# A four-layer graph network on one core: projections of layer 0's second step taken before its weighted sums, another split of the first group, and later projections in layers 1 and 2

## The chip, the core and the metric

The kernel runs on one core of a Trainium2 chip. The core has five engines that work side by side, each through its own instructions in order: TensorE (PE, matrix products and transposes), VectorE (DVE), ScalarE (ACT), GpSimd (POOL), and SyncE (SP), which here issues every transfer between the chip's memory and the core. An instruction that waits holds up all that stands behind it on its engine, and the same is true of SP's queue of transfers.

The metric is the time of one execution on the device in microseconds. The kernel before took 3104.74 us, the median of three runs (3103.69, 3104.74 and 3111.75).

## The reference

A graph of 3327 nodes with 256 features and a weighted adjacency matrix goes through four layers, each `x = x + layer(relu(layernorm(x)), adj)`. The change is mainly in layer 0:

```python
R = S + eye; R = R / R.sum(-1, keepdims=True)
Z = 0; Xf = X; Xa = X
for n in range(2):
    A = top_p_attention(Xa, W1, W2, W3)   # row softmax, the largest entries up to mass 0.9, renormalised
    Xf = R @ Xf
    Xa = A @ Xa
    Z = Z + Xf @ U1[n].T + Xa @ U2[n].T
h = X + Z
return layernorm(h) * ln_g + ln_b
```

Layer 1 is `relu(tanh(adj * adj) @ (tanh(h @ W_proj + b) @ W_gcn) + b_gcn)`, the mask and the limit of 700 entries a row changing nothing for such data. Layers 2 and 3 are graph attention: `Wh = h @ W`, scores from two columns of `Wh @ a`, a softmax over the neighbours, and a product with `Wh`. Everything is float32.

## The kernel before

The nodes are padded to 26 tiles of 128 rows. The matrix `adj` is at hand as it is and as transposed blocks `adj_t`.

**Layer 0** (function `layer0`) runs its two steps one after the other, and in each step the 26 tiles in nine groups of up to three (`FG`). For a group (function `group`):

- *Scores*: eight matrix products a tile (L1042) with the keys `kt` and a query that SP loads from `q_d`; DVE copies them from PSUM with a running maximum (L1016), ACT takes the exponential (L1025).
- *Threshold search*: a first guess (L1085 on DVE), then four rounds. In a round the mass above a candidate threshold is summed over a whole row of 3328: on DVE in one pass (L1131), or on ACT in two (L1126, Relu and Sign, with sums). `ON_ACT = [2, 2, 1, 2]` says how many of the three tiles ACT takes in each round. Some ten small DVE operations (L1137 to L1158) then give the next threshold.
- *Final*: two more DVE passes and a maximum of eight a tile (L1173, L1176, L1187).
- `weighted` for each tile: transposes of the probabilities (L951), copies by ACT (L953), 26 products with the rows `xa` (L941) into `ps_out`; ACT multiplies by the norm (L963). The result and the row of `R @ Xf`, loaded from `xf_d` as `xf_in`, are transposed (`turned`, L785, L786) and multiplied with `u1s` and `u2s` (L971) into `ps_row`; DVE adds what the row has so far (`h` in step 1, `base_row` loaded from `zz_d` in step 2, L979) and the sum is stored to `zz_d`. In step 1 the transposed result also gives the keys and query of step 2 (`keys_of`, L858). Also in step 1, a triple that depends on nothing of it: a tile of `x` is loaded, the bias `ln_b` is added on POOL, and the sum is stored to `xb_d` for layer 1 (L989 to L991, one buffer).

Beside the groups run the *neighbour tiles* (`neighbours`): four block loads of `adj_t` a tile (L906), 26 products (L915) into the single `ps_acc`, a scaling on ACT (L923), a store to `xf_d` or `xf2_d`. In step 1 ACT also takes the sign of each block (L909, one buffer `sg`) and SP stores it to `sign_d` for the later layers. Step 2 takes its `xf` from `xf_d` by two large loads (L1230).

All of this is written as Python generators. `overlapped` starts a new group every 20 ticks and advances every running generator by one `yield` a tick; a scheduler then places the instructions engine by engine by its own model of their times, so that program order and engine order differ. In the first group of a step no other group is at hand to fill in.

**Layer 1** goes over the 26 tiles: two block loads, a DVE and an ACT pass, 26 products (L1482), then `summed` for the tile before and `entered2` for the one before that, which is `Entry.tile_in`: normalise on ACT (L1400), transpose on PE (L785), copy by ACT (L786), product with `w2l` (L1405), two copies (L1409, L1410). `Entry.__init__` computes a bound of the scores (`shift`) on PE, DVE and POOL (L1376 to L1385). Layers 2 and 3 are two calls of `attention`; while layer 2 runs, works in `todo` do the same `tile_in` for layer 3.

Of the kernel before, what the change touches and what calls it, by code (L numbers as in the profile page):

```python
# [20 lines left out]
P = 128  # L21
# [45 lines left out]
def kernel(  # L67
# [107 lines left out]
    xf2_d = dram.tile([NP, D], F32, name="xf2_d")  # L175
    xb_d = dram.tile([NP, D], F32, name="xb_d")
# [569 lines left out]
    def layers(fast):  # L746
# [54 lines left out]
        def layer0(wp, mp, ap_, tp, sp):  # L801
# [43 lines left out]
            def u_tiles(s):  # L845
                pair = []
                for u, name in ((u1t, "u1s"), (u2t, "u2s")):
                    t = wp.tile([P, 2, D], F32, tag=name, name=name)
                    nc.sync.dma_start(t, u[s].rearrange("(c p) n -> p c n", p=P))
                    pair.append(t)  # L850
# [31 lines left out]
            for span in spans:  # L882
# [7 lines left out]
                for k, it in enumerate(span):  # L890
# [3 lines left out]
                    keys_of(turned(row, "xt", 2), 0, it)  # L894
# [4 lines left out]
            def neighbours(s, it, xf):  # L899

                acc = ps_acc()
                w = XW if s == 0 else D
                for chunks in QB:
# [3 lines left out]
                    if s == 0:  # L907
                        sg = tp.tile([P, 7, P], I8, tag="sg", bufs=1, name="sg")
# [14 lines left out]
                nc.scalar.mul(row, acc[:, :D], rr[:, it : it + 1])  # L923
                nc.sync.dma_start((xf_d, xf2_d)[s][it * P : (it + 1) * P, :], row)
                yield

            def weighted(s, it, e, norm, xa, xa_next, us):

                if s == 0:
                    base = h(it)[:, :D]  # L930
                else:
                    base = tp.tile([P, D], F32, tag="base", bufs=1, name="base_row")
                    nc.sync.dma_start(base, zz_d[it * P : (it + 1) * P, :])
                xf_in = tp.tile([P, D], F32, tag="xf_in", name="xf_in")
# [24 lines left out]
                if s == 0:  # L959
                    row = xa_next(it)[:, :D]  # L960
                else:
                    row = tp.tile([P, D], F32, tag="xa_row", bufs=1, name="xa_row")
                nc.scalar.mul(row, po, norm)  # L963
                yield
                xt = turned(row, "xt", 2)
                xft = turned(xf_in, "xft", 2)
                yield
                pz = ps_row()
                for n, (lhs, u) in enumerate(((xft, us[0]), (xt, us[1]))):
# [5 lines left out]
                if s == 0:  # L975
                    keys_of(xt, 1, it)
                yield
                zrow = tp.tile([P, D], F32, tag="zrow", bufs=1, name="zrow")
                nc.vector.tensor_tensor(zrow, pz[:, :D], base, ALU.add)  # L979
                nc.sync.dma_start(zz_d[it * P : (it + 1) * P, :], zrow)  # L980
                if s == 1:
                    norm_of(zrow, sp, "mv_z", mv_z[:, it, :])
                yield
                if s == 0:

# [467 lines left out]
        with tc.tile_pool(name="l1", bufs=2, reuse_waits="tile") as l1:  # L1453
# [15 lines left out]
            for it in range(NT):  # L1469
# [17 lines left out]
                if it >= 2:  # L1487
                    entered2(it - 2)
# [246 lines left out]
```

## Time and profile before

| | |
|---|---|
| median of three runs | 3104.74 us |
| the profiled execution, its own time | 3100.91 us |
| its span, first to last instruction | 3099.1 us |
| layer 0, step 1: last product with `h` ends | about 1017 us |
| layer 0, step 2: last product with `xa` ends | about 1999 us |
| layer 1: products with `gw` | about 1999 to 2343 us |
| layers 2 and 3 | about 2343 to 3099 us |
| mean granted clock of TensorE | 0.973 |

The profile is one execution on the chip. It has the busy time of each engine; the span in 40 slices, each digit the busy tenths of one slice; the chain of work that ended last, followed back from the end; groups of instructions by source line; and waits by who released them. The times of the trace are microseconds from the start of the span. In lines of instructions the first number is the start, the second the length, then engine, line, operation, output and inputs; what stands in brackets is the idle time before, and what ended it. Each matrix product in float32 shows as two records, so that 26 products count as 52.

### The profile page before, as it was taken

To read this page: it belongs to the slowest core of one execution; us is meant where nothing else is said; L and a number is where in the kernel's file an instruction comes from. 1 tells how busy PE (TensorE), PEld (TensorE's weight loads), DVE (VectorE), ACT (ScalarE), POOL (GpSimd) and SP (SyncE) were. 2 spreads that over 40 slices of the span, in tenths; PEclk is the share of its full clock that TensorE was granted. 3 is DMA by queue.
4 is the path that set the end of the run, shared out by engine and by line. 5 is a ranking of instruction groups with operands and counts; after the bars stand their busy time and mean duration, and the time that the engine had idled before them with its cause. 6 is when DMAs were issued, how large, how long until landed. Compare 5 with 4: busy or idle time off the path is not lost.

```text
span 3099.1 us, 37681 instructions
## 1 busy us (share of the span) xinstructions
PE 2823.0 (91%) x13454; PEld 2277.8 (73%) x13454; DVE 2370.4 (76%) x4133; ACT 1979.7 (64%) x2633; POOL 417.8 (13%) x742
## 2 busy tenths in 40 slices
PE   7788899999999899999999988999997999979998
PEld 5466677777778576667777767888886887758887
DVE  3678889778874588889876858377765999769996
ACT  6767787768773566687666555433334777657776
POOL 0120010000001001111110024211110333210000
PEclk9889999999999999999999989999998999989999
DMA  4431112321242231211232231388871211112221
GB/s 138 131 102 45 55 45 76 95 78 57 75 121 87 73 103 53 64 35 54 74 90 72 83 114 60 105 321 318 324 243 32 71 59 59 30 48 78 75 74 37
DMA packets 183035, 298.83 MB, mean 96 GB/s; under 512 B 24701, under 2 KB 137016, under 8 KB 179512
## 3 DMA queue, kind: packets, MB, share of 16 engines
q1 hardware_dynamic: 182838, 296.34, 30.3%
q8 instruction: 108, 1.77, 0.3%
q14 instruction: 89, 0.72, 0.1%
HBM read 251.97 MB, written 44.30 MB: 96 GB/s over the span
## 4 chain that ended last, share of the span: by engine, by line
DVE 38%; PE 27%; ACT 16%; issue 8%; DMA 7%; POOL 3%; SPq 0%; ACTq 0%; POOLq 0%; DVEq 0%
ACT junk_a L1126 9%; PE ps_wide L1594 5%; DVE below L1173 4%; PE ps_out L941 4%; PE ps_acc L915 4%; DVE w L1176 4%; PE ps_wide L1482 4%; DVE below L1131 3%; DVE e L1187 3%; DVE places L1601 3%; DVE places L1587 2%; DVE below L1085 2%; DVE places L1588 2%; DMA blk<-in_adj_t 2%; DMA adj_rows<-in_adj 2%
## 5 line engine op out<-in xcount | busy, mean ns | idle before, releaser
L1126 ACT ACTIVATE junk_a<-e,minus 128x3328 int8<-128x3328 f32 x208 | 638.8, 3071 | 3.7
L1594 PE MATMUL ps_wide<-wh,places 128*128 128x257 f32 x1872 | 451.2, 383 | 35.6 <-DVE places L1588 32.7
L1594 PEld LDWEIGHTS ps_wide<-wh,places 128*128 128x128 f32 x1872 | 353.3, 191 | 93.6 <-ACT places L1586 16.5
L915 PE MATMUL ps_acc<-h,blk 128*128 128x258 f32 x1352 | 333.3, 399 | 46.8 <-ACT xf_row L923 37.1
L915 PEld LDWEIGHTS ps_acc<-h,blk 128*128 128x128 f32 x1352 | 261.8, 198 | 102.3 <-ACT xf_row L923 42.7
L1016 DVE TENSOR_SCALAR_CACHE_REDUCE e<-ps_wide 128x1024 f32<-128x1024 f32 (+1 forms) x176 | 178.6, 1019 | 206.9 <-PE ps_wide L1042 206.4
L915 PE MATMUL ps_acc<-xf,blk 128*128 128x256 f32 x1352 | 312.9, 384 | 14.3 <-ACT xf_row L923 14.2
L941 PE MATMUL ps_out<-h,wt 128*128 128x256 f32 x1352 | 311.2, 381 | 4.7 <-ACT wt L953 4.7
L941 PE MATMUL ps_out<-xa,wt 128*128 128x256 f32 x1352 | 311.9, 381 | 0.9 <-ACT wt L953 0.7
L1585 ACT ACTIVATE places<-places,sd 128x512 f32<-128x512 f32 (+1 forms) x364 | 246.3, 684 | 100.5 <-PE ps_wide L1594 67.6
L1482 PE MATMUL ps_wide<-gw,blk 128*128 128x256 f32 x1352 | 300.9, 379 | 1.3 <-ACT blk L1479 1.3
L915 PEld LDWEIGHTS ps_acc<-xf,blk 128*128 128x128 f32 x1352 | 253.9, 191 | 61.8 <-ACT xf_row L923 19.3
L1482 PEld LDWEIGHTS ps_wide<-gw,blk 128*128 128x128 f32 x1352 | 254.5, 190 | 35.0 <-ACT blk L1479 1.7
L941 PEld LDWEIGHTS ps_out<-h,wt 128*128 128x128 f32 x1352 | 249.8, 190 | 40.1 <-ACT wt L953 6.3
L941 PEld LDWEIGHTS ps_out<-xa,wt 128*128 128x128 f32 x1352 | 249.4, 190 | 34.8 <-ACT wt L953 3.0
L1586 ACT ACTIVATE places<-places,d 128x512 f32<-128x512 f32 (+1 forms) x364 | 235.8, 682 | 48.7 <-DVE places L1587 48.2
L1131 DVE SCALAR_TENSOR_TENSOR below<-e,v 128x3328 f32<-128x3328 f32 x72 | 265.3, 3684 | 1.8
L1587 DVE TENSOR_TENSOR places<-places,places 128x1024 f32<-128x1024 f32 (+1 forms) x182 | 210.2, 1163 | 65.8 <-ACT places L1585 63.7
L1042 PE MATMUL ps_wide<-keys,q 64*128 64x512 f32 (+1 forms) x832 | 215.9, 570 | 17.8 <-DVE e L1016 14.8
L953 ACT COPY wt<-ps_wide 128x1024 f32<-128x1024 f32 x208 | 175.2, 846 | 86.2 <-PE ps_wide L951 85.6
L1588 DVE SCALAR_TENSOR_TENSOR places<-blk_s,places 128x1024 f32<-128x1024 int8 (+1 forms) x182 | 206.3, 1142 | 2.0
L1176 DVE MAX8 w<-below 128x8 f32<-128x3328 f32 x52 | 188.3, 3621 | 0.3
(275 smaller groups left out, 4312.6 us busy)
## 6 DMA issues: line engine op xcount, KB each, us to landing
blk<-in_adj_t SPq DMA_DIRECT2D x104, 448.0 KB, 3.5
blk<-in_adj_t SPq DMA_DIRECT2D x52, 832.0 KB, 7.1
adj_rows<-in_adj SPq DMA_DIRECT2D x25, 1663.5 KB, 8.4
blk<-in_adj_t SPq DMA_DIRECT2D x104, 384.0 KB, 3.3
blk_s<-sign_d SPq DMA_DIRECT2D x72, 256.0 KB, 2.9
blk_s<-pos_d SPq DMA_DIRECT2D x44, 416.0 KB, 3.6
pos_d<-pos SPq DMA_DIRECT2D x22, 416.0 KB, 2.9
xf_d<-xf_row SPq DMA_DIRECT2D x52, 128.0 KB, 2.4
```

The source lines that it names most:

```text
L915: nc.tensor.matmul(acc[:, :w], blk[:, j, :], xf(jc)[:, :w], start=(jc == 0), stop=(jc == NT - 1))
L941: nc.tensor.matmul(po, wt[:, k * P : (k + 1) * P], xa(jc)[:, :D], start=(jc == 0), stop=(jc == NT - 1))
L1042: nc.tensor.matmul(pl[:, f * 512 : f * 512 + cw], q[f * DA : (f + 1) * DA, :], kt[f * DA : (f + 1) * DA, s, c0 : c0 + cw], start=True, sto ...
L1126: nc.scalar.activation(junk, es[i], (AF.Relu, AF.Sign)[n], bias=minus[:, 0, i : i + 1], accum_out=(ga, sa)[n][:, 0, i : i + 1],)
L1131: nc.vector.scalar_tensor_tensor(below, es[i], v[:, 3, i : i + 1], es[i], ALU.is_ge, ALU.mult, accum_out=v[:, 1, i : i + 1],)
L1176: nc.vector.max(w9[:, i, 1:9], below)
L1482: nc.tensor.matmul(po, filt[:, j * P : (j + 1) * P], gw(jc), start=(jc == 0), stop=(jc == NT - 1))
L1585: nc.scalar.activation(e1[:, :, q, :], s0, AF.Exp, bias=sd[:, jc + q, 1:2])
L1586: nc.scalar.activation(e2[:, :, q, :], s1, AF.Exp, bias=d2[:, jc + q : jc + q + 1])
L1587: nc.vector.tensor_tensor(e1, e1, e2, ALU.max)
L1588: nc.vector.scalar_tensor_tensor(e1, signs[:, :n, j : j + 2, :], 0.0, e1, ALU.is_gt, ALU.min)
L1594: nc.tensor.matmul(pos_[k], e1[:, k, q, :], wh(jc + q)[:, : D + 1], start=(jc + q == 0), stop=(eye and jc + q == NT - 1),)
```

## The change

In step 1, `weighted` now multiplies the transposed rows also with the U1 and U2 of step 2 (a second product `py`), stores the one result to `xfu_d` and keeps the other as the rows `xa` of step 2; both pairs of U stay in memory. Step 2 then needs no transposes and no projection: `neighbours` adds the row of `zz_d` to its scaled row on POOL, and `weighted` ends with one DVE operation, `po * norm + xf_in`. The xb triple moves to the end of `neighbours` in step 2. The signs have two buffers, `xt`, `xft` and `xf_in` one each. In a step's first group ACT takes at most one tile a round. `Entry.tile_in` is split into `turned` and `projected`, with a tile between them; the score bound becomes a method, `shifted`, called later.

```diff
             def neighbours(s, it, xf):
...
+                if s == 1:
+                    base = tp.tile([P, D], F32, tag="xf_in", bufs=1, name="base_row")
+                    nc.sync.dma_start(base, zz_d[it * P : (it + 1) * P, :])
...
-                        sg = tp.tile([P, 7, P], I8, tag="sg", bufs=1, name="sg")
+                        sg = tp.tile([P, 7, P], I8, tag="sg", name="sg")
...
                 nc.scalar.mul(row, acc[:, :D], rr[:, it : it + 1])
+                if s == 1:
+                    nc.gpsimd.tensor_tensor(row, row, base, ALU.add)
                 nc.sync.dma_start((xf_d, xf2_d)[s][it * P : (it + 1) * P, :], row)
                 yield
+                if s == 1:
+                    xb = tp.tile([P, D], F32, tag="xt", bufs=1, name="xb")
+                    r = rows_of(it)
+                    for a, b in rows_to_load(it):
+                        nc.sync.dma_start(xb[a:b], x[it * P + a : it * P + b])
+                    nc.gpsimd.tensor_tensor(xb[:r], xb[:r], b_b[0][:r], ALU.add)
+                    nc.sync.dma_start(xb_d[it * P : it * P + r, :], xb[:r])

             def weighted(s, it, e, norm, xa, xa_next, us):
...
+                zrow = tp.tile([P, D], F32, tag="zrow", bufs=1, name="zrow")
+                if s == 1:
+                    yield
+                    nc.vector.scalar_tensor_tensor(zrow, po, norm, xf_in, ALU.mult, ALU.add)
+                    nc.sync.dma_start(zz_d[it * P : (it + 1) * P, :], zrow)
+                    norm_of(zrow, sp, "mv_z", mv_z[:, it, :])
+                    yield
+                    return
...
-                for n, (lhs, u) in enumerate(((xft, us[0]), (xt, us[1]))):
+                for n, (lhs, u) in enumerate(((xft, us[0][0]), (xt, us[0][1]))):
...
+                py = ps_row()
+                for n, (lhs, u) in enumerate(((xft, us[1][0]), (xt, us[1][1]))):
+                    for cc in range(2):
+                        nc.tensor.matmul(
+                            py[:, n * D : (n + 1) * D], lhs[:, cc, :], u[:, cc, :], start=(cc == 0), stop=(cc == 1)
+                        )
                 yield
+                row = tp.tile([P, D], F32, tag="xf_row", name="xfu_row")
+                nc.scalar.copy(row, py[:, :D])
+                nc.sync.dma_start(xfu_d[it * P : (it + 1) * P, :], row)
+                nc.scalar.copy(xa_next(it), py[:, D:])
+                yield
...
-                    on_act = list(range(max(g - ON_ACT[r], g - 2 if g > 2 else 1), g)) if g > 1 else []
+                    most = 1 if tiles[0] == 0 else ON_ACT[r]
+                    on_act = list(range(max(g - most, g - 2 if g > 2 else 1), g)) if g > 1 else []
...
-                nc.sync.dma_start(t, xf_d[f * HB * P : (f + 1) * HB * P, :].rearrange("(t p) d -> p t d", p=P))
+                nc.sync.dma_start(t, xfu_d[f * HB * P : (f + 1) * HB * P, :].rearrange("(t p) d -> p t d", p=P))
...
                 if it >= 2:
-                    entered2(it - 2)
+                    entry2.turned(it - 2, xn(it - 2))
+                if it == 2:
+                    entry2.shifted()
+                if it >= 3:
+                    projected(it - 3)
...
-                    rest = [lambda it=it: following.tile_in(it, xn(it)) for it in span]
-                    todo += [stats[:2]] + [rest[k : k + 1] + stats[k + 2 : k + 3] for k in range(n)]
-                    todo.append([lambda i=i: following.spread(i)])
+                    turned = [lambda it=it: following.turned(it, xn(it)) for it in span]
+                    made = [lambda it=it: following.projected(it) for it in span]
+                    todo += [stats[:2]] + [
+                        turned[k : k + 1] + made[max(k - 1, 0) : k] + stats[k + 2 : k + 3] for k in range(n)
+                    ]
+                    todo.append(made[-1:] + [lambda i=i: following.spread(i)])
```

## The prediction

> **What bounds the kernel now.** I read the page's busy shares and slices first, then busy time in stretches of the run, then single rounds.
>
> ```profile
> PE 2823.0 (91%) x13454; PEld 2277.8 (73%) x13454; DVE 2370.4 (76%) x4133; ACT 1979.7 (64%) x2633; POOL 417.8 (13%) x742
> ...
> PE   7788899999999899999999988999997999979998
> ...
> PEclk9889999999999999999999989999998999989999
> ...
> DVE 38%; PE 27%; ACT 16%; issue 8%; DMA 7%; POOL 3%; SPq 0%; ACTq 0%; POOLq 0%; DVEq 0%
> ```
>
> TensorE is busy 2823 of 3099 us; 276 us are idle, gathered where a stage starts (the low digits, with a lower clock). The busy times between ends of groups in layer 0 (start:end, length, then PE, PEld, DVE, ACT, POOL):
>
> ```profile
> 266.00:359.00 93.00, 81.41 (x396) 61.70 (x396) 80.86 (x157) 71.88 (x77) 3.00 (x17) 0.96 0.15 43
> ...
> 560.00:665.00 105.00, 99.36 (x486) 77.42 (x485) 82.58 (x159) 78.51 (x83) 3.39 (x18) 0.98 0.26 75
> ...
> 1197.00:1290.00 93.00, 87.14 (x420) 66.51 (x420) 81.75 (x161) 66.10 (x63) 12.31 (x23) 0.98 0.19 55
> ...
> 1478.00:1579.00 101.00, 95.61 (x470) 74.57 (x469) 87.47 (x169) 67.16 (x65) 15.28 (x25) 1.00 0.23 66
> ```
>
> A group with three neighbour tiles in it is bound by PE at 95% busy; one with fewer (the first and third row) is held by DVE and PE together. So time that leaves PE counts in full only until DVE (81 to 87 us a group) is the bound. The start of step 2, one round (start, length, engine):
>
> ```profile
> 1074.80 3.69 DVE L1131 SCALAR_TENSOR_TENSOR below<-e,v 128x3328 f32<-128x3328 f32 x1
> ...
> 1088.94 0.16 DVE L1137 SCALAR_TENSOR_TENSOR sa<-sa,v 128x2 f32<-128x2 f32 x1 [8.87 <-ACT junk_a L1126]
> ```
>
> ```profile
> 1076.18 3.06 ACT L1126 ACTIVATE junk_a<-e,minus 128x3328 int8<-128x3328 f32 x1
> ...
> 1079.36 3.07 ACT L1126 ACTIVATE junk_a<-e,minus 128x3328 int8<-128x3328 f32 x1
> ...
> 1082.55 3.07 ACT L1126 ACTIVATE junk_a<-e_h,minus 128x3328 int8<-128x3328 f32 x1
> ...
> 1085.75 3.07 ACT L1126 ACTIVATE junk_a<-e_h,minus 128x3328 int8<-128x3328 f32 x1
> ```
>
> With no other group to fill in, the round is four ACT passes (13 us), while DVE does one pass and waits 8.87 us.
>
> **The first group's split (both steps).** One tile of three goes to ACT: two passes, 6.4 us, beside two DVE passes, 7.4, plus 1.9 of small operations: 9.3 us a round. In step 1 the rounds now start at 106.8, 133.0, 150.4 and 160.3 and end at 177.5. The first also holds group 1's exponentials: 26 becomes 12, the second 17.4 becomes 9.4, the third (already one) stays, the last 17 becomes 9.4. That is -30, and -2 for scores that no longer queue behind the xb transfers: the first product moves from 203.7 to about 172. In step 2 (rounds from 1056.8 to 1115.3) the gains are 4, 5, 0 and 6 us, less 3 to 5 because the second half of `xf` now waits for the last tile's projected row: -12.
>
> **What that start gives back.** In the built order of the changed kernel only 4.0 neighbour tiles stand before PE's first product in step 1; before it was 6.35, and by the ninth product the counts agree (9.8). A tile is 52 matmuls of 0.217 us, 11.3 us. So 2.35 tiles, 26.6 us of PE, move from the idle start into the PE-bound part: +28 at 95%. In step 2 it is 5.3 against 6.3, made up by the twelfth product.
>
> **Projections in step 1.** Each tile gains four matmul pairs. Their rows of step 2:
>
> ```profile
> 1152.23 0.44 PE L785 MATMUL ps_row<-ident,xa_row 128*128 128x128 f32 x2
> 1152.51 0.38 PE L785 MATMUL ps_row<-ident,xf_in 128*128 128x128 f32 x2
> ...
> 1158.21 1.13 PE L971 MATMUL ps_row<-u1s,xft 128*128 128x256 f32 x4
> 1159.18 1.03 PE L971 MATMUL ps_row<-u2s,xt 128*128 128x256 f32 x4
> ```
>
> 2.16 us x 26 = 56 us of PE, 59 at 95%. The idle left in 203 to 457 (23 us, of which 13 stay at 5%) takes up 10 to 13. The two new ACT copies a tile (0.4 us as the 128x256 copies, 22 in all) lie beside PE, ACT being at 75%; without that cover they are late releases of PSUM. The new product needs a `ps_row` bank that DVE's zrow addition frees, and that can stand behind a 3.7 us pass: 0 to +15; PE waits there are under 2 us each today, so I take +3. The extra `xfu_d` stores (2.4 us like `xf_d`) are needed only at the step's end. **Step 1: -32 +28 +59 -12 = +43.**
>
> **Step 2 without them.** Each tile loses all four rows above: 2.98 us x 26 = 77 us of PE, plus the waits for `xa_row` and `xft` (9.5 us between 1190 and 1720). DVE's work stays (one operation replaces the addition). Groups in turn, DVE taken at 94% busy, as it is between 2400 and 2600 (91.8 and 95.3) where it bounds: after the first product 62 loses 3; 93, 93 become 87 (DVE 82/0.94), -6 each; 95 gets 0.8 of a neighbour tile more, -1; 101 becomes 93 (DVE 87.5), -8; 126 and 113, PE-bound, -9 each; 121 is partly the latency of the last group and layer 1's entry, -4; the last 60, -5. With the 12: **step 2: -63.**
>
> **The xb stream.** Its 26 load-add-store triples sat in the start of step 1 on one buffer; now they stand in SP's queue at the start of step 2, about one per two block loads.
>
> ```profile
> SPq L991 <- POOL xb L990: 40.2, 14, 5.6
> ```
>
> SP waited 40 us for these additions (14 times, 5.6 at most); queued behind are block loads and thus PE. In step 1's start neighbour tiles came every 14 to 25 us, with the single-buffered signs as a second cause (now two buffers); undisturbed, every 12. In step 2 the 4.3 tiles before the first product have from about 1046 to 1121 by the old clock, room for 17 us each. Ends: 0, or 4.3 x 7 = +30. Nearer the undisturbed row, as no sign stores stand between: +4.
>
> **Additions on POOL.** 26 new row+base additions. The Trainium skill, "GPSIMD Engine Reference", sections 4.1 and 8, advises against: a two-input operation takes about twice VectorE's time and contends with VectorE instructions that have two SBUF inputs. Here the same addition takes 0.73 us (median of 26), but up to 3.04; the DVE pass at 202.03, beside one, took 4.02 against 3.69. By time on POOL, 13% busy, the sum is 0; with that 0.33 each, +9. I take +1.
>
> **The clock.** "TensorE: Matmul & The Clock Gate", Part 1, says that PE halves its clock after about 3.4 us idle and needs as much work to return: 1.7 us lost each time. It speaks against an emptier start. The row: a neighbour tile after 4.6 us idle (177.7) took 14.3 us, after 1.7 us (1103.8) 11.5. Three returns cost 8 by the trace, 5 by the rule; the four or five of today go, and the start's end is set by DVE: 0.
>
> **Later projections.**
>
> ```profile
> PE ps_row L1405 <- ACT ht L786: 10.6, 10, 2.6
> ```
>
> In layer 1 (1990 to 2330) PE, 95% busy, waits ten times for the copy of a transposed tile, 10.6 us in all. A tile's delay removes it; next to be late is the 85 to 90% busy DMA: ends 0 and -11, I take -6. In layer 2 the same wait is 8.0 us, but DVE bounds: -2 with the moved `shifted`. Both transitions (2330 to 2370, 2730 to 2765) keep their chain. Layer 3: 0. `b_b`, both u loads and the tag changes lie in idle DMA: 0.
>
> **Sum.** +43 +3 -63 +4 +1 -6 -2 = -20. The profiled execution took 3100.9 us (span 3099.1), 3.8 under the median of the runs, 3104.7. 3101 - 20 = 3081; I say 3082.
>
> **Rivals.**
> 1. *Step 1 absorbs the projections.* If the 59 us fill PE's waits (ACT is asked less in the starts, signs have two buffers, and PE idles 5% even in the full groups) half of it vanishes, -50 in all: 3050. For it: waits for `xf_row` and `xa` of 37 us in 266 to 1000. Against: these come from in-order ACT queues, which get longer.
> 2. *A wash.* Step 2 proves DVE-bound at 90 a group and the deferred tiles cost all: the -63 becomes -44, 3101.
> 3. *Slower: the xb stream stalls SP at step 2's start.* Were neighbour tiles there at 20 us or more, the first product waits for PE's queue, not for DVE: from 17 us a tile on, each microsecond costs 4.3. At 25, as the worst tile of step 1's start, (25 - 17) x 4.3 = 34 over my sum, 3115; with a bank wait of 8 in step 1, 3123.
> 4. That an edit does nothing is excluded: the built order has the 104 transposes fewer and the products moved.
>
> **Numbers.** Forecast 0.53, first rival 0.29, wash 0.09, slower 0.09. A difference under 0.3% (9 us) can't be told from none. Of the forecast 0.52 lies beyond that on the faster side and 0.01 within; of the wash 0.03 and 0.06; of the slower case 0.01 within and 0.08 beyond. Faster: 0.52 + 0.29 + 0.03 = 0.84; same 0.01 + 0.06 + 0.01 = 0.08; slower 0.08. The range reaches from the first rival, with 5 us for its bounds, 3045, to where half of the slower case begins, 3108.
>
> **What would show it.** Right: step 1's last product near 1060 (now 1016), 26 products of step 2 in about 63 us less than now; first-group rounds of 9 to 12 us; PE groups of about 110 us in step 1 and 87 to 94 in step 2; no PE wait for `ht`. Wrong: step 1 ending before 1045, SP waits for xb above 40 us together with PE waits for `blk` in step 2, or step 2 groups still at 93.

## The result, and the profile after

The changed kernel takes 3088.44 us (median of six runs, 3087.45 to 3093.37), the kernel before 3104.77 us (six runs beside it, 3101.63 to 3111.75). The ratio is 0.9946, with a 95% interval of 0.9935 to 0.9957: some 16 us or 0.5% faster. The forecast was 3082, 20 us under the profiled execution of before. The profiled spans are 3099.1 and 3086.4 us, 12.7 apart; the sums below are made against these spans.

The page of the kernel after: busy times, then PE and the granted clock of PE over 40 slices, then the shares of the chain that ended last.

```profile
PE 2806.9 (91%) x13350; PEld 2274.9 (74%) x13350; DVE 2405.2 (78%) x4145; ACT 1932.0 (63%) x2583; POOL 433.7 (14%) x768
...
PE   7789999999999978989999988999997999979998
...
PEclk9889999999999999999999999999998999989999
...
PE 22%; DVE 18%; issue 5%; ACT 4%; DMA 3%; POOL 2%; SPq 0%; ACTq 0%; DVEq 0%; POOLq 0%
```

PE's busy time fell by 16 us only (2823.0 to 2806.9), and at the start of step 2 its digits are lower than before (7898 from the 15th slice on, where the kernel before has 9999 behind a single 8). The chain now adds up to 54% of the span: its links end halfway, so it is not read here.

The busy times by stage say more. The rows are: products of step 1 (first to last), the gap to the first product of step 2, products of step 2. Columns: start:end, length, then busy time of PE, PEld, DVE, ACT, POOL, granted clock, DMA share, GB/s. Before:

```profile
203.70:1016.80 813.10, 762.17 (x3759) 603.97 (x3759) 628.48 (x1199) 586.48 (x634) 42.12 (x135) 0.98 0.24 71
1016.80:1135.10 118.30, 105.22 (x459) 75.04 (x459) 80.05 (x189) 69.14 (x60) 11.58 (x23) 0.97 0.39 109
1135.10:1999.00 863.90, 800.01 (x3990) 639.39 (x3990) 678.71 (x1344) 556.38 (x606) 142.76 (x251) 0.98 0.24 70
```

After:

```profile
168.90:1050.20 881.30, 836.83 (x4077) 667.20 (x4077) 632.54 (x1201) 607.39 (x692) 36.46 (x136) 0.98 0.24 73
1050.20:1168.00 117.80, 94.11 (x415) 65.38 (x415) 96.06 (x195) 50.78 (x49) 37.30 (x44) 1.00 0.49 146
1168.00:1994.50 826.50, 755.66 (x3746) 604.44 (x3746) 689.90 (x1361) 532.12 (x532) 173.22 (x285) 0.97 0.27 79
```

Step 1 starts its products 34.8 us earlier and then needs 68.2 more for them. The gap between the steps kept its length, though PE does 11 us less in it. Step 2's products need 37.4 less. Behind layer 0 another 8.2 us went (1100.1 to 1091.9): -34.8 + 68.2 - 0.5 - 37.4 - 8.2 = -12.7.

The single groups after, the second and the fifth of each step, as in the four rows that the prediction shows of before:

```profile
233.00:340.00 107.00, 102.47 (x501) 80.58 (x502) 87.34 (x160) 78.64 (x88) 5.82 (x17) 0.98 0.24 69
...
562.00:676.00 114.00, 107.29 (x509) 83.69 (x508) 82.90 (x159) 80.19 (x89) 3.43 (x18) 0.96 0.25 72
...
1227.00:1317.00 90.00, 80.82 (x391) 62.07 (x390) 83.51 (x161) 63.19 (x53) 16.29 (x25) 0.98 0.21 61
...
1505.00:1604.00 99.00, 91.87 (x442) 71.39 (x441) 84.44 (x166) 65.41 (x55) 14.87 (x26) 0.98 0.24 71
```

The groups of step 1 are now PE-bound: 94 to 96% busy in the two shown, 95% over the stage. A group of step 2 with two neighbour tiles takes 90 us with DVE 93% busy (83.5), one with three 99.

Layer 1 gained too. PE's first product after the transition to layer 2 starts at these times before and after; layer 0 ended 4.5 us earlier, so 9 of the 13.5 us are layer 1's, and layers 2 and 3 take as long as before (728.4 and 729.2 us from here to the end).

```profile
2370.68 1.62 PE L1594 MATMUL ps_wide<-wh,places 128*128 128x257 f32 x3 [8.54 <-DVE places L1588]
```

```profile
2357.22 3.34 PE L1624 MATMUL ps_wide<-wh,places 128*128 128x257 f32 x7 [8.54 <-DVE places L1618]
```

### The profile page after: what moved, and what is told of

It reads as the page before. It is cut to its first block, busy times and chain, and to the rows that moved or that the text cites. A ratio compares the mean times of both kernels' runs of the same rounds, so it can differ in the third digit from the quotient of the medians.

```text
span 3086.4 us, 37597 instructions
## 1 busy us (share of the span) xinstructions
PE 2806.9 (91%) x13350; PEld 2274.9 (74%) x13350; DVE 2405.2 (78%) x4145; ACT 1932.0 (63%) x2583; POOL 433.7 (14%) x768
## 4 chain that ended last, share of the span: by engine, by line
PE 22%; DVE 18%; issue 5%; ACT 4%; DMA 3%; POOL 2%; SPq 0%; ACTq 0%; DVEq 0%; POOLq 0%
PE ps_wide L1624 6%; PE ps_wide L1505 6%; DVE places L1631 3%; PE ps_out L951 3%; DVE places L1617 3%; DMA adj_rows<-in_adj 3%; DVE places L1618 2%; PE ps_acc L919 2%; ACT junk_a L1141 2%; DVE below L1146 1%; PE ps_acc L1624 1%; PE ps_out L1624 1%; DVE below L1188 1%; DVE w L1191 1%; PE ps_row L1428 1%
## 5 line engine op out<-in xcount | busy, mean ns | idle before, releaser
L1141 ACT ACTIVATE junk_a<-e,minus 128x3328 int8<-128x3328 f32 x196 | 601.8, 3070 | 4.3
L1146 DVE SCALAR_TENSOR_TENSOR below<-e,v 128x3328 f32<-128x3328 f32 x78 | 288.5, 3698 | 1.8
L951 PEld LDWEIGHTS ps_out<-h,wt 128*128 128x128 f32 x1352 | 250.4, 191 | 37.4 <-ACT wt L963 3.4
L1038 ACT ACTIVATE e<-e,nm 128x3327 f32<-128x3327 f32 x44 | 134.9, 3067 | 102.7 <-DVE nm L1037 102.7
```

Source lines behind the costliest of these rows:

```text
L951: nc.tensor.matmul(po, wt[:, k * P : (k + 1) * P], xa(jc)[:, :D], start=(jc == 0), stop=(jc == NT - 1))
L1141: nc.scalar.activation(junk, es[i], (AF.Relu, AF.Sign)[n], bias=minus[:, 0, i : i + 1], accum_out=(ga, sa)[n][:, 0, i : i + 1],)
L1146: nc.vector.scalar_tensor_tensor(below, es[i], v[:, 3, i : i + 1], es[i], ALU.is_ge, ALU.mult, accum_out=v[:, 1, i : i + 1],)
```

## The gap between the steps: what the profile shows

The prediction took 12 us off this gap for the even split, and it is as long as it was. (A round is counted from one first pass of VectorE over the row, L1131 before and L1146 after, to the next.) Where the second round of the first group ends, VectorE (start, length, operation, idle time before it and who ended it) has this, in the kernel after:

```profile
1106.39 3.69 DVE L1146 SCALAR_TENSOR_TENSOR below<-e,v 128x3328 f32<-128x3328 f32 x1
...
1123.90 0.16 DVE L1091 SCALAR_TENSOR_TENSOR a<-mu 128x3 f32<-128x3 f32 x1 [6.56 <-POOL mu L1041]
...
1124.97 3.69 DVE L1146 SCALAR_TENSOR_TENSOR below<-e,v 128x3328 f32<-128x3328 f32 x1
```

and POOL, in the same microseconds:

```profile
1116.38 0.72 POOL L929 TENSOR_TENSOR xf_row<-xf_row,base_row 128x256 f32<-128x256 f32 x1
1123.00 0.72 POOL L938 TENSOR_TENSOR xb<-xb,b_b 128x256 f32<-128x256 f32 x1 [5.89 <-DMA xb<-in_x]
1123.68 0.19 POOL L1041 TENSOR_TENSOR mu<-e,nm 128x1 f32<-128x1 f32 x1
```

The round lasts 18.6 us instead of some 11. DVE waits for `mu`, a POOL operation of 0.2 us that belongs to the next group's scores. `mu` stands in POOL's queue behind an addition of the xb stream, and that one waits 5.9 us for its load. The load in turn stands in SP's queue, where the single xb buffer must first be stored:

```profile
SPq L939 <- POOL xb L938: 54.9, 19, 5.5
```

(engine and line, what it waited for: us in all, times, the longest; 1020 to 1240.) The even split did shorten the rounds. The stream, moved to this place, took it back. Two in-order queues stand in a row here: the load is late in SP's, and what is behind it is late in POOL's. This is a reading; the experiments below put a price on the stream, but none of them parts the two queues.

## Experiments

**1. The even first groups undone.**

```diff
-                    most = 1 if tiles[0] == 0 else ON_ACT[r]
+                    most = ON_ACT[r]
```

> The change with its even first groups undone (first groups give two of three tiles to ACT again); everything else stays. Theory A (the shared row buffers): the 2.35 neighbour tiles that left the start of step 1 did so because the row buffers are shared, not because the first group is short; in the built order this kernel still has 4.0 tiles ahead of the first product. So the split is a pure gain of some 30 us in step 1 and a few in step 2's start: first product of step 1 near 198 (after: 169), time 3088 + 28 to 34 = about 3119. Theory B (the prediction's sum: what the short start gains, it gives back as deferred tiles): +4 in step 1, at most +12 in step 2: 3092 to 3104. Theory C (the early first product comes from the xb stream's leaving step 1, not from the split): first product near 178, 3092 to 3098.

3117.2 us, ratio 1.0045 (1.0031 to 1.0058): theory A. The first product comes at 190.3, 21 us later than with the split; the gap between the steps grows to 130 us. TensorE and VectorE in the first group's last rounds (window of busy times, then VectorE's lines):

```profile
140.00:166.00 26.00, 0.00 (x0) 0.00 (x0) 14.85 (x33) 22.80 (x19) 0.48 (x1) 0.52 0.07 26
```

```profile
141.16 0.16 DVE L1152 SCALAR_TENSOR_TENSOR sa<-sa,v 128x2 f32<-128x2 f32 x1 [4.11 <-ACT junk_a L1141]
...
165.16 0.16 DVE L1152 SCALAR_TENSOR_TENSOR sa<-sa,v 128x2 f32<-128x2 f32 x1 [9.30 <-ACT junk_a L1141]
```

The waits of 4 and 9 us for ACT's passes are back, and PE does nothing for 26 us: its four neighbour tiles are done and no more are placed before the first product. In the kernel before, the longer rounds had 6.35 tiles beside them. So here the slow start brings no neighbour tile forward in return: its 21 us are lost whole. The first product at 190, 13 us ahead of before (203.7) with the same split, also says that a part of the early start is owed to something else.

**2. The split and the later projections alone.** Before's projections in both steps and its xb stream in step 1, with the two other edits of the change.

```diff
-                    on_act = list(range(max(g - ON_ACT[r], g - 2 if g > 2 else 1), g)) if g > 1 else []
+                    most = 1 if tiles[0] == 0 else ON_ACT[r]
+                    on_act = list(range(max(g - most, g - 2 if g > 2 else 1), g)) if g > 1 else []
...
-            def tile_in(self, it, src):
+            def turned(self, it, src):
...
+            def projected(self, it):
```

> The kernel before with only the even first groups and the later projections; rows are multiplied by U1 and U2 in both steps as before. In the built order 5.0 neighbour tiles stand ahead of step 1's first product and 5.2 in step 2. Theory A (the prediction's terms: what multiplying early costs in step 1, +59 -12 +3, is what it saves in step 2, -51 +5, so that it is a wash or a loss of up to a deferred tile): 3088 -4 -12 to 3088, about 3080, faster than or equal to the full change. Theory B (the pre-multiplication carries the gain): 3088 + 10 or more, 3098 to 3104, with step 2 groups at 93 again and first product near 175.

3089.8 us, ratio 0.9953 (0.9935 to 0.9972), the same as the full change within the intervals. Multiplying early, the change's largest edit, moves the time by nothing that can be told. Its stages:

```profile
183.20:1014.00 830.80, 781.35 (x3825) 620.50 (x3826) 630.81 (x1200) 593.01 (x641) 46.85 (x140) 0.98 0.25 74
1014.00:1117.30 103.30, 92.55 (x401) 64.18 (x400) 90.15 (x195) 50.04 (x47) 13.55 (x22) 0.97 0.37 103
1117.30:1993.80 876.50, 815.14 (x4049) 654.61 (x4049) 678.92 (x1344) 557.25 (x606) 136.40 (x252) 0.97 0.24 71
```

Read against the two tables above: the split alone brings the first product from 203.7 to 183.2 and the gap from 118.3 to 103.3, and pays 18 us in step 1's products and 13 in step 2's, where its deferred tiles land (1.3 and 1.15 of them in the built order, at 11.3 us). The early multiplication then adds 50.5 us to step 1's products and takes 50.0 from step 2's; it takes 14.3 from step 1's start, where the stream is gone, and adds 14.5 to the gap, where it has arrived. Behind layer 0 this kernel is only 2.6 us shorter than before (1097.5), though it has the same later projections with which the full change is 8.2 shorter.

**3. Rows in another buffer.** The change keeps the new rows `xa_row` and `xfu_row` in the two `xf_row` buffers, in turn with the neighbour tiles' rows.

```diff
-                row = tp.tile([P, D], F32, tag="xf_row", name="xa_row")
+                row = tp.tile([P, D], F32, tag="zrow", bufs=1, name="xa_row")
...
-                row = tp.tile([P, D], F32, tag="xf_row", name="xfu_row")
+                row = tp.tile([P, D], F32, tag="zrow", bufs=1, name="xfu_row")
```

> The change, but the two new rows of a tile (xa_row, xfu_row) sit in the zrow buffer instead of the two xf_row buffers that the neighbour tiles use. In the built order 5.04 neighbour tiles then stand ahead of step 1's first product instead of 4.0. Theory A (a deferred tile costs PE time in the PE-bound part): 1.04 tiles x 11.3 us = -12, 3076, with the first product still near 169 to 172. Theory B (PE's idle 5% absorbs a deferred tile, or the tile placed in the start holds up the first product by as much): 3086 to 3090.

3075.7 us, ratio 0.9910 (0.9896 to 0.9924): theory A, 12.8 us under the full change. The window ahead of the first product after, and then in this kernel:

```profile
140.00:166.00 26.00, 12.01 (x55) 10.46 (x54) 25.45 (x45) 8.65 (x9) 3.52 (x6) 0.76 0.30 87
```

```profile
140.00:166.00 26.00, 23.24 (x111) 19.52 (x110) 25.45 (x46) 11.63 (x15) 4.12 (x7) 0.98 0.57 163
...
166.70:1034.90 868.20, 821.88 (x4021) 654.66 (x4022) 634.83 (x1203) 607.15 (x690) 35.69 (x135) 0.98 0.24 71
```

PE does one neighbour tile more (11 us) in a time in which it stood idle, DVE and the rounds are untouched, and the products of step 1 take 868 us instead of 881. With two shared buffers the fifth tile's row gets its turn only behind `xa_row` of the first product, whatever the split. Against experiment 2 (ratio 0.9953) this kernel is 14 us faster, with intervals that lie apart: with the rows out of the neighbour tiles' buffers, multiplying early, and what goes with it, is a gain.

**4. One tile more.** On top of experiment 3, step 1's first group asks for its neighbour tiles from its first round on.

```diff
-                first = 2 if g == len(todo) else 0
+                first = 2 if g == len(todo) and tiles[0] else 0
```

> The change with the new rows in the zrow buffer, and the first group of step 1 asks for its neighbour tiles from its first round on, not from its third: in the built order 6.04 tiles then stand ahead of step 1's first product (row_in_zrow: 5.04; after: 4.0). In row_in_zrow PE does 8.3 of 20 us between 100 and 120 and stands idle from 107 to 120. Theory A (each tile placed in that gap takes 11 to 12 us out of the PE-bound part): 3076 - 11 = 3065, first product still near 167. Theory B (the extra tile's loads and ACT passes hold the rounds or the first product up by as much): first product near 175, 3073 to 3078.

3078.9 us, ratio 0.9919 (0.9907 to 0.9932): no gain, theory B in sum, though not by its mechanism alone. The first product comes at 170.6 instead of 166.7, and the second group then has less to fill it. The window 230 to 330 in experiment 3 and here:

```profile
230.00:330.00 100.00, 93.34 (x460) 71.08 (x458) 85.85 (x170) 79.09 (x85) 3.13 (x21) 0.98 0.18 51
```

```profile
230.00:330.00 100.00, 87.47 (x421) 67.05 (x420) 81.76 (x157) 74.08 (x82) 4.11 (x16) 0.93 0.11 35
```

The second group has 0.8 neighbour tiles in it instead of 1.5 and lasts 2 us longer (96 instead of 94): here a tile taken out of a group that has only one or two is no gain.

**5 to 10. The xb stream.** Six kernels price it.

*Without it in the kernel before*, and *without it on top of experiment 3*. Both leave out the addition of ln_b, which is all zeros with these inputs:

```diff
-                    xb = tp.tile([P, D], F32, tag="xt", bufs=1, name="xb")
...
-                    nc.sync.dma_start(xb_d[it * P : it * P + r, :], xb[:r])
...
-                    nc.sync.dma_start(xs_(it)[a:b], xb_d[it * P + a : it * P + b])
+                    nc.sync.dma_start(xs_(it)[a:b], x[it * P + a : it * P + b])
```

> The kernel before without the xb stream: layer 1's entry loads x itself, and the addition of ln_b (all zeros with these inputs) is left out. With the split undone the changed kernel's first product came at 190, 14 us ahead of the kernel before; with only the split and the stream left in step 1's start it came at 183, 14 us behind the full change. Both differ from their neighbours by the xb stream and by the second buffer for the signs. Theory A (the stream costs step 1's start 14 us by itself; the prediction had 2): first product 188 to 192 (before: 203.7), start of step 2 still 118, time 3104 - 12 to 15 = 3089 to 3092. Theory B (it was the single buffer of the signs that held the neighbour tiles there): first product 200 to 203, 3100 to 3104.

3094.65 us, ratio 0.9975 (0.9965 to 0.9985). The first product comes at 191.4, 12 us earlier: theory A for the start. In all 7 us stay in the median, 4 in the profile: step 1's products take 3.5 us more, the gap and step 2 the same as before, and the part behind layer 0 is 5 longer (1105 instead of 1100). The other kernel:

> row_in_zrow without any xb stream: layer 1's entry loads x itself, and the addition of ln_b (all zeros with these inputs) is left out. It is the floor of what moving the stream can bring. Moving it into the entry shortened the start of step 2 by 12 us and lengthened the entry by 16; pacing it shortened the start by 11 and lengthened the groups by 11. Theory A (the additions and the stream cost wherever they stand): start of step 2 (row_in_zrow: 117.5) near 106, groups of step 2 at row_in_zrow's lengths, time 3076 - 12 = 3064. Theory B (an earlier first product of step 2 is given back in any case, because DVE-bound groups or layer 1's entry set the end): start near 106, last product of step 2 near 1983 as in row_in_zrow, 3074 to 3077.

3066.0 us, ratio 0.9875 (0.9860 to 0.9890): theory A. The gap between the steps is 106 us (experiment 3: 117.5), and step 2's products take as long as there (829 and 831), so the gain of the gap is kept through step 2. Behind layer 0 it is 4 us longer (1095 and 1091), as before_no_xb is. Its first group's rounds start at

```profile
1077.36 3.69 DVE L1138 SCALAR_TENSOR_TENSOR below<-e,v 128x3328 f32<-128x3328 f32 x1
...
1089.31 3.69 DVE L1138 SCALAR_TENSOR_TENSOR below<-e,v 128x3328 f32<-128x3328 f32 x1
...
1100.57 3.69 DVE L1138 SCALAR_TENSOR_TENSOR below<-e,v 128x3328 f32<-128x3328 f32 x1
...
1111.76 3.69 DVE L1138 SCALAR_TENSOR_TENSOR below<-e,v 128x3328 f32<-128x3328 f32 x1
```

12.0, 11.3 and 11.2 us apart, and the fourth ends 9.3 us on at 1121.1: 43.7 us, where the full change needs 52.9 (1094.2 to 1147.1). The difference of 9.2 is most of the 12; 6.6 of it is the one wait for `mu`. What splitting the first group evenly gains here is thus the 15 us that the prediction took for it (rounds of 58.4 us before).

*The additions in layer 1's entry*, on the full change: the entry loads x into its own rows and adds ln_b there.

```diff
-                    nc.sync.dma_start(xs_(it)[a:b], xb_d[it * P + a : it * P + b])
+                    nc.sync.dma_start(xs_(it)[a:b], x[it * P + a : it * P + b])
+                r = rows_of(it)
+                nc.gpsimd.tensor_tensor(xs_(it)[:r], xs_(it)[:r], b_b[0][:r], ALU.add)
```

> The change without the xb stream: layer 1's entry loads x into its own rows and adds ln_b there on POOL, so 26 load-add-store triples leave the start of step 2. Theory A (SP's waits for the xb additions and POOL's waits for their loads are what ate the 12 us that the even split should have gained at the start of step 2): last product of step 1 to first of step 2 falls from 118 to 106 to 110, time about 3077. Theory B (the start is set by the chain of rounds and by the late second half of xf; the stream hides): 118 stays, 3086 to 3090.

3095.1 us, ratio 0.9970 (0.9959 to 0.9980): neither. The gap fell to 106 us as theory A has it, and the time rose by 7. The waits between 1820 and 1945 in this kernel, one of POOL's lines, and the wait of the full change at the same place (1830 to 1936):

```profile
PE ps_row L786 <- ACT temps L1292: 26.9, 1, 26.9
```

```profile
1849.40 9.75 POOL L1280 TENSOR_TENSOR xs<-xs,b_b 128x256 f32<-128x256 f32 x9
```

```profile
PE ps_row L786 <- DMA xs<-xb_d: 12.4, 1, 12.4
```

With no buffer to hold them back the scheduler put nearly all the additions into POOL's queue at once, ahead of the small POOL operations (`mv`) that the first entry needs. ACT, and behind it PE's in-order queue, waited 26.9 us instead of 12.4. That is the gain of the gap and more.

*Paced*, on the full change: one triple a product, in the zrow buffer.

```diff
+                if s == 1:
+                    xb = tp.tile([P, D], F32, tag="zrow", bufs=1, name="xb")
...
+                    nc.gpsimd.tensor_tensor(xb[:r], xb[:r], b_b[0][:r], ALU.add)
+                    nc.sync.dma_start(xb_d[it * P : it * P + r, :], xb[:r])
```

> The change with the xb triples moved from the start of step 2 to one per product of step 2: a tile's xb sits in the zrow buffer, so that it can't run ahead of the products. The run that moved the additions into layer 1's entry shortened the start of step 2 from 118 to 106 us and lost it at 1820 to 1942 (122 us instead of 106 between the 21st and 24th product). Theory A (the stream costs 12 us only where it crowds the start; spread over the groups it hides): start of step 2 about 106, groups as after (90, 91, 99, 101, 116, 106, 106, 59), 3076. Theory B (POOL additions and SP stores cost the same wherever they are): start 106, groups longer by 12 in sum, 3088. A small rise of 1 us a tile in the groups would be 26 and put it above 3100.

3087.0 us, ratio 0.9945 (0.9932 to 0.9958): theory B. The gap is 108 us, the products take 837 instead of 827. SP's queue of transfers waited for the additions between 1240 and 2000:

```profile
SPq L945 <- POOL xb L944: 58.8, 18, 6.9
```

*The store from POOL's queue*, first with the stream where the change put it, then paced, both on top of experiment 3:

```diff
-                    nc.sync.dma_start(xb_d[it * P : it * P + r, :], xb[:r])
+                    nc.gpsimd.dma_start(xb_d[it * P : it * P + r, :], xb[:r])
```

> row_in_zrow with the 26 xb stores issued from POOL's queue, behind the addition on the same engine, instead of from SP's. SP no longer waits for the additions (53 us in 18 waits between 1020 and 1240), only for the free buffer. Theory A (SP's waits in front of the neighbour tiles' loads are what makes the start of step 2 long): start 117.5 falls to 106 to 111, 3064 to 3070. Theory B (POOL's own queue is what counts: a round's tail waited 6.6 us for a POOL addition of the exponentials' chain that stood behind an xb addition): start 116 to 119, 3073 to 3080, more if issuing a store takes POOL long.

3080.9 us, ratio 0.9926 (0.9912 to 0.9940): theory B in time, and the gap is 120 us. SP no longer waits for additions (53 us in experiment 3), but it waits all the longer for the single buffer, which is free only when POOL's store has landed: 99 us between 1020 and 1240, where experiment 3 has 29.

```profile
SPq L937 <- DMA xb_d<-xb: 99.2, 22, 7.4
```

VectorE's wait is the same, and POOL ahead of it:

```profile
1107.35 0.16 DVE L1091 SCALAR_TENSOR_TENSOR a<-mu 128x3 f32<-128x3 f32 x1 [6.30 <-POOL mu L1041]
```

```profile
1105.51 0.72 POOL L938 TENSOR_TENSOR xb<-xb,b_b 128x256 f32<-128x256 f32 x1 [2.88 <-DMA xb<-in_x]
1106.53 0.56 POOL L939 DMA_DIRECT2D xb_d<-xb  x1 [0.30 <-POOL xb L938]
1107.11 0.20 POOL L1041 TENSOR_TENSOR mu<-e,nm 128x1 f32<-128x1 f32 x1
```

`mu` again comes right behind an addition that waited for its load. So this kernel does not decide between SP's queue and POOL's: it left both as full as they were.

> row_in_zrow with the xb triples one per product of step 2 and the stores on POOL's queue. xb_paced, with the stores on SP, gave back 11 us in the groups, where SP waited 59 us in 18 waits for the additions. Theory A (these SP waits were the price): start near 106, groups at row_in_zrow's lengths, 3064 to 3067. Theory B (the price is the addition itself on POOL, beside DVE passes and ahead of POOL's small operations): 3073 to 3077, as row_in_zrow.

3071.15 us, ratio 0.9892 (0.9877 to 0.9907). The gap is 108 us, the products 834 (experiment 3: 831). It lies between the theories: some 10 us of the 12 that the stream costs in the gap by zrow_no_xb are gone, 3 to 4 come back in the groups, and 3 behind layer 0 (1094 and 1091). Its interval and that of experiment 3 overlap, so that the 4.5 us between them are likely, not certain. This is the fastest kernel here that computes everything: 33 us or 1.1% under the kernel before, twice the change's gain, with three edits to it.

**11. The base addition on VectorE.**

```diff
-                nc.scalar.mul(row, acc[:, :D], rr[:, it : it + 1])
-                if s == 1:
-                    nc.gpsimd.tensor_tensor(row, row, base, ALU.add)
+                if s == 1:
+                    nc.vector.scalar_tensor_tensor(row, acc[:, :D], rr[:, it : it + 1], base, ALU.mult, ALU.add)
+                else:
+                    nc.scalar.mul(row, acc[:, :D], rr[:, it : it + 1])
```

> The change with the 26 new row+base additions of step 2 moved from POOL into one VectorE operation (acc * rr + base), which also takes 26 multiplications from ACT. Theory A (the prediction: the POOL additions cost about 1 us, and DVE is not the bound in step 2 but in the first groups): 3085 to 3092. Theory B (the additions on POOL stretch DVE passes by 0.33 us each, and the long chain ACT, POOL, DMA holds up ps_acc, for which PE waits 18 us between 1200 and 1700): 3075 to 3080. Theory C (DVE bounds the groups with few neighbour tiles, 26 x 0.5 us more on it show): 3095 to 3102.

3099.4 us, ratio 0.9975 (0.9965 to 0.9985): slower than the full change by 11 us, theory C in size, but by another mechanism. (The profiled execution is the slowest of 13, which range from 3090.5 to 3106.2; its span is 18 us over the full change's.) VectorE is no busier in the group shown (83.9 us as in the row at 1317 below); what changed is who releases `ps_acc`. The windows, then PE's waits in them, here:

```profile
1320.00:1419.00 99.00, 89.37 (x418) 69.12 (x417) 83.89 (x168) 68.27 (x54) 12.47 (x21) 0.93 0.21 59
```

```profile
PE ps_acc L919 <- DVE xf_row L928: 8.8, 2, 6.0
```

and in the full change:

```profile
1317.00:1408.00 91.00, 81.95 (x391) 63.09 (x391) 83.79 (x162) 64.24 (x53) 16.70 (x25) 0.96 0.19 55
```

```profile
PE ps_acc L919 <- ACT xf_row L927: 5.0, 1, 5.0
```

The next neighbour tile needs the single `ps_acc`, and DVE's operation that frees it stands behind passes of 3.7 us. These waits, the 27 PE records more (half a tile) that fall into this group, and a lower granted clock (0.93 and 0.96 in the rows) go with its 8 us. The half tile comes from the gap, where 4.9 neighbour tiles were done before the first product instead of 5.3, at a granted clock of 0.92 instead of 1.00. A full account of the 11 us was not made. The edit moves two things at once, the addition from POOL and the scaling from ACT, and so the release of `ps_acc`. The Trainium skill advises to keep such additions off POOL ("GPSIMD Engine Reference", sections 4.1 and 8); this fused form on VectorE is slower here, and a plain addition on VectorE behind ACT's scaling was not run.

**12. The later projections undone.**

```diff
-                        turned[k : k + 1] + made[max(k - 1, 0) : k] + stats[k + 2 : k + 3] for k in range(n)
+                        turned[k : k + 1] + made[k : k + 1] + stats[k + 2 : k + 3] for k in range(n)
...
-                if it >= 3:
-                    projected(it - 3)
+                    projected(it - 2)
```

> The change with the later projections of layers 1 and 2 undone (a tile is turned and projected in the same turn, the shift is computed at construction). Theory A (the prediction's terms -6 and -2, and the 8.2 us measured behind layer 0): 3088 + 8 = 3096, with PE waiting some 10 us for ht in layer 1 again. Theory B (DMA in layer 1 is late next, so the wait only changes its name; the 8.2 us come from the odd microseconds of other stages): 3088 to 3091.

3099.5 us, ratio 0.9983 (0.9976 to 0.9989): theory A, 11 us, of which the profile shows 6 behind layer 0; the other 4 to 5 lie in layer 0, which the edit does not touch, so a few microseconds in a stage of a single profile are not to be put down to an edit. PE's waits in layer 1 (1995 to 2340):

```profile
PE ps_row L1429 <- ACT ht L787: 11.0, 11, 2.1
```

The waits for the transposed tile are back. In the full change 0.9 us of them are left, and the largest wait there is another one of four times:

```profile
PE ps_row L1445 <- ACT sd L1432: 7.9, 4, 4.8
```

## The prediction, term by term

The sum came out near the measured time, within its range, but in part by luck: the terms below miss by -3, +3, -13, +7.5, +13, 0, -3 and +3 us, and a cost of 13 that was not there hides one of 13 that was not foreseen. Of the signs that the prediction named, those of step 1 came roughly true (last product at 1050, full groups of 107 to 115 us), and so did the end of the wait for `ht`. In step 2 they did not: with its gap it became 38 us shorter, not 63, and a round of its first group took 18.6 us. The sign of being wrong there, SP waiting over 40 us for xb together with PE waits for `blk`, came true as well (54.9 and 9.4 us between 1020 and 1240).

Measured sizes come from the stage tables: the split from before to experiment 2, the early multiplication from experiment 2 to after, the shared rows from after to experiment 3.

| term | predicted, us | measured, us |
|---|---|---|
| step 1, first product | -32 | -35 |
| step 1, deferred tiles | +28 | +31 (18 by the split, 13 by the shared rows) |
| step 1, projections: 59 - 12 + 3 | +50 | +37 |
| gap between the steps: -12 + 4 for the stream | -8 | -0.5 (-15 and +14.5) |
| step 2, deferred tiles | 0 | +13 |
| step 2 without projections: -51 + 1 | -50 | -50 |
| layer 1; layers 2 and 3 | -6; -2 | -9; +1 |
| sum | -20 | -12.5 |

- **First product.** The sum was right, its parts were not. The prediction had -30 for the shorter rounds and -2 for the xb stream. The split is worth 21 and the stream's departure 12 to 14 (before without the stream: 191.4; the change without the split: 190.3). With one sign buffer (before_no_xb) or two (no_split) the time is nearly the same, so the second buffer adds little once the stream is gone. The prediction read the stream as queue time of the scores on SP. The trace of before shows another path, also through SP's queue. SP issued the store of a sign at 105.06, 1.2 us after ACT had made it, behind an xb store that waited for POOL and behind a block load; without the stream it was issued at once. ACT waited for the landing, in its one sign buffer, ahead of the first round's passes, and began these some 3 us later in the round. In before, and then in before_no_xb:

```profile
109.31 0.95 ACT L909 ACTIVATE sg<-blk 128x896 int8<-128x896 f32 x1 [5.45 <-DMA sign_d<-sg]
```

```profile
102.31 0.95 ACT L909 ACTIVATE sg<-blk 128x896 int8<-128x896 f32 x1 [1.82 <-DMA sign_d<-sg]
```

VectorE waited for `mu` only 1.4 us in that start, so it isn't the path of step 2. The first round is 4 us shorter without the stream (22.0 and 26.2); the other 8 are spread over the start, and what makes them is not shown.
- **Deferred tiles in step 1.** 2.35 tiles at 11.3 us were counted rightly from the built order. The reason given, that the short start leaves room for fewer, holds for 1.3 of them. The other 1.04 tiles follow from the change of buffers, which the prediction costed at nothing with "the tag changes lie in idle DMA": a buffer shared by two chains is an order between them.
- **Projections in step 1.** The term that was mis-sized is 2.16 us a tile. It added the lengths of two rows, 1.13 and 1.03, whose ends overlap: by 0.217 us a record, the size it used two paragraphs above, eight records are 1.74 us, 45 us in all. (The Trainium skill, "TensorE: Matmul & The Clock Gate", Part 2, has the rule: the drain of one product overlaps the filling of the next, so a product in a stream costs less than one alone; the rows agree, with 0.28 us a record in a row of four and 0.22 in one of 52.) PE's busy time rose by 40.5 (781.4 to 821.9). The "absorbed 10 to 13" was the error in the other direction: PE's idle time in the stage went from 49.4 to 46.3 us, so 3 were absorbed. The +3 for a bank wait is inside the 37 and was not measured by itself. The 77 us of step 2 are mis-summed in the same way: PE's busy time there fell by 59.5 (815.1 to 755.7); the sum did not use them, as it took the groups one by one.
- **The gap.** The step that failed here is "nearer the undisturbed row, as no sign stores stand between: +4". The stream costs 14.5 there (10 to 12 by the kernels without it). The prediction looked for its price in SP's queue and in PE's block loads. The waits it named did come (SP 54.9 us in the start, PE 9.4 us for `blk`), but what lengthens the chain of rounds is largely a step behind them, in POOL's queue, where `mu` waits behind a late addition and stops VectorE for 6.6 us in one round. Whether the additions would hurt there with their loads in time is not shown. The -12 for the split was sound: 15 without the moved stream, 12 by undoing the split.
- **Step 2's deferred tiles.** "Made up by the twelfth product" put them at nothing. They are made up inside groups that are bound by PE and DVE at once, and cost 13 us, as much as in step 1.
- **Step 2's groups.** 87, 87, 94 and 93 were predicted and 90, 91, 97 and 99 measured. The two short ones are DVE's, as said: 83.5 us busy at 93%. The others carry the deferred tile.
- **POOL additions** at +1 and the **later projections** within their bounds: as said. The wait for `ht` went, and layer 1 gained 9 of at most 11; 7 come back in layer 1 when the projections are undone (no_later), but experiment 2 gained only 3 there with the same edit, so not all of the 9 is shown to be theirs.
- **The clock** at 0: the mean is 0.970 after 0.973. The 1.7 us that the prediction has for a return is an estimate (half of its 3.4); its two tiles differ by 2.8.

Of the rivals, the first (step 1 absorbs half of the projections) fell: 3 us, not half of 59. The third had the right place but not its size or its mechanism. The second, a wash, is right in sum for the early multiplication as it was built, against experiment 2, and the change is faster by the split and the later projections. With the rows out of the neighbour tiles' buffers (experiment 3) it gains 14 us.

What stays open: why the part behind layer 0 grew by 4 to 5 us in both kernels without the stream; how much of layer 1's 9 us the later projections gave; how the price of the stream at step 2's start divides between SP's queue and POOL's; and the whole of the 11 us of base_on_dve.

## What to carry to other kernels

Work that is moved out of one stage's start is worth nothing until it has somewhere to go: the 26 small triples cost 12 us at either start (7 and 10 in the whole time), 15 in the entry behind, 11 when paced with stores on SP, and least, 4, when paced with the stores off SP's queue. Ask of each moved operation what waits behind it in its engine's in-order queue, the 0.2 us operations above all. And a temporary that takes a buffer of another chain orders the two chains: one 1 KB row per partition, shared here, cost a whole neighbour tile of 11 us in the place where PE was idle.

## What was not expected of the hardware

Beside VectorE's passes over a row, by the profile (which calls spans on POOL rough), small POOL operations stretch far beyond their own time, and not the other way round by as much: the 128x256 addition takes 0.72 us alone and up to 4.0 beside a pass, the 128x128 addition 0.45 and up to 3.9, while the pass itself goes from 3.69 to between 3.9 and 4.2. That this is time and not only a rough span shows in zrow_pool_store: an addition of 3.99 us began at 1090.87, and the store that waits for it on the same engine at 1095.16. The store itself occupied POOL for 0.56 us a piece, where SP needs 0.33 for the same transfer.
